# The end of an attention layer in a new order, and six of its sixteen output groups moved into the next layer's first steps

## The chip, the cores and the metric

The kernel runs on one core of a Trainium2 chip. The metric is device time in microseconds (us) of one launch. The engines are TensorE (PE for matmuls, PEld for weight loads), VectorE (DVE), ScalarE (ACT), GpSimd (POOL) and SyncE (SP, which issues the DMAs). All data is fp32.

## The reference

Four layers, each a gated cross-attention and a gated feed-forward network, are applied in turn to `x`, 128 batches of 64 tokens with 128 features (8192 tokens). The change lies between the two halves of layer 2 (the third layer):

```
x = x + tanh(g_xattn[2]) * L2_xattn(layernorm(x), ctx)     # 16 heads of 8, softmax over 64 keys
x = x + tanh(g_ffn[2])   * L2_ffn(layernorm(x))            # 32 experts

# L2_xattn:
q, k, v = x @ Wq + bq, ctx @ Wk + bk, ctx @ Wv + bv
attn = softmax(clip(q k^T / sqrt(8)))
attn = 1/64 everywhere if any attn is nan
out  = (attn v) @ Wo + bo

# L2_ffn: a sigmoid router picks 2 of 4 groups of experts, then the 8 best experts of these
final  = sum over chosen experts of w_e * down_e(silu(gate_e x) * up_e x)
shared = down_s(silu(gate_s x) * up_s x)
```

## The kernel before

`x` stays in SBUF for the whole kernel as 64 tiles of 128 tokens. A *pair* is two tiles (256 tokens, 32 pairs, numbers `u`), a *group* four tiles (512 tokens, 16 groups, numbers `g`). Group `g` holds pairs `2g` and `2g+1`.

The order of the instructions is written out by hand. Every engine is wrapped in `InOrder` (line 158), whose `issue` ties each instruction to the one issued before on that engine; so an engine runs its instructions in the order in which the Python code emits them, and all instructions carry line 166 in the profile. Work is told apart by the names of its tiles.

Layers are generators. While one layer ends, it calls `ahead().step()`, which runs the next layer's generator up to its next `yield`: this is how the first work of the next layer is put between the last work of this one. After a `yield False` a step does nothing more.

`l2_cross` (line 745) is the attention. Its `period(i)` (line 927) emits one step of a software pipeline over pairs by `PLAN` (line 920): scores, clamp, maximum, exponentials, `turn` (transposes of the attention, tile `aT`), `values` and `place` (the values into `vz`), `heads` (attention times values and the denominators, tile `pso_l2x`) and `divide` (a reciprocal and a product on DVE into `oT_all`). The tail begins when all 32 pairs have had their scores:

- `check` (line 949) counts NaNs in a sum of exponentials and leaves the flag `bad`. It needs all pairs' scores, so nothing may leave before it.
- `leave(g)` (line 958) is a `copy_predicated` on DVE, which puts the mean of the values into the group's part of `oT_all` where `bad` is set, and four 128x128 matmuls (two passes each) with `Wo` into a PSUM bank `psf`.
- `add(g)` (line 967) is one DVE instruction that adds the gated `psf` to `x`.
- `groups(lo, hi)` (line 971) emits `leave` for a run of groups, `add` two groups behind, and one `ahead().step()` after each add.

The three last `period` calls finish pairs 29, 30 and 31, with groups 0 to 4, 5 to 9 and 10 to 15 between and after them.

`l2_ffn` (line 990) is the expert layer. Its steps ahead are, for group 0: `statistics`, `norm`, `transposes`, `logits`, `sigmoid`, `groups`, `best_groups`, `best_experts`, `shares` and `spread` (the expert weights are transposed as `pswt`, copied as `wT` and written to DRAM by four DMAs, `wrow`), and then `statistics(1)` and `norm(1)`. The main part (line 1155) begins with `fetch(0)`: eight DMAs that spread the weights over all partitions as four 1 MB blocks `wb`, each for four steps. Then for every group there are 17 steps `j`, each with two experts (64 hidden features each), the last with the shared one:

- `hidden(g, j)`: the gate and up matmuls into a double bank `psgu` (two such buffers exist);
- `gated(g, j)`: `sl` on ACT (Silu), `uw` on DVE (up times weight `wb`), `h` on POOL (their product);
- `down(g, j-2)`: the down matmul into `psy`.

Between the steps stand the next group's router by the plan in line 1139 (`j` = 2 to 9) and the statistics of the group after it (`j` = 12 and 14). PSUM has four single banks (`psf`, `psy`, `psx`, `pswt`, ...) and two double ones. The buffers `sl`, `h`, `uw` take SBUF which `oT_all` had, so the first of them waits for its last use.

Of the kernel before, what the change touches and what calls it, by code (L numbers as in the profile page):

```python
# [9 lines left out]
F32 = mybir.dt.float32  # L10
U8 = mybir.dt.uint8
U32 = mybir.dt.uint32
AF = mybir.ActivationFunctionType
ALU = mybir.AluOpType
AX = mybir.AxisListType

P = 128
NB, SQ, DM = 128, 64, 128
DC = 96
NTOK = NB * SQ  # L20
NT = NTOK // P
NP = NT // 2
NG = NT // 4
# [31 lines left out]
def flamingo_kernel(ctx: ExitStack, tc: tile.TileContext, a: dict, out: bass.AP):  # L55
# [118 lines left out]
    def opened(name, bufs=1, side=None):  # L174
        pl = tc.tile_pool(name=name, bufs=bufs, side=side, reuse_waits="tile")
        return pl
# [17 lines left out]
    class Heads:  # L194
# [24 lines left out]
        def values(self):  # L219
            self.v = v = self.new("v", [P, 4, 256], bufs=3)  # L220
            for half in range(2):
                ps = bank(f"psv_{self.name}_{half}")
                for i in range(2):
                    b0 = self.p * 256 + (half * 2 + i) * SQ
                    for r in range(2):
                        self.pe.matmul(ps[r * 64:(r + 1) * 64, i * 256:(i + 1) * 256], lhsT=ctxT[0:self.vrows, b0:b0 + SQ],
                                       rhs=self.w["v"][0:self.vrows, self.off + r * 256:self.off + (r + 1) * 256],
                                       start=True, stop=True)
                self.act.copy(v[:, 2 * half:2 * half + 2, :].rearrange("p a b -> p (a b)"), ps)
# [39 lines left out]
        def power(self):  # L269
            s16 = self.s.rearrange("p a r k -> p (a r) k")  # L270
            self.act.activation(s16, s16, AF.Exp)

        def divide(self):
            s16 = self.s.rearrange("p a r k -> p (a r) k")
            den, rec = self.new("den", [P, 16]), self.new("rec", [P, 16])
            self.dve.tensor_reduce(den, s16, AX.X, ALU.add)
            self.dve.reciprocal(rec, den)
            self.at = self.s if self.null is None else self.new("at", [P, 8, 2, 64])
            self.pool.tensor_tensor(self.at.rearrange("p a r k -> p (a r) k"), s16[:, :, 0:64], bc(rec, 2, 64), ALU.mult)
# [462 lines left out]
                        W["l1x"] = weights("l1x", sp)  # L742


    def l2_cross(ahead):

        stack = ExitStack()
# [165 lines left out]
        def divide(u):  # L913
            rec = wk2.tile([P, 256], F32, tag="rec", name=f"rec_l2x_{u}", bufs=1)
            dve.reciprocal(rec, su[u]["o"][:, 256:512])
            dve.tensor_tensor(oT[:, u * 256:(u + 1) * 256], su[u]["o"][:, 0:256], rec, ALU.mult)
            su[u].clear()


# [7 lines left out]
        def period(i):  # L927
            for kind, lag, f, *more in PLAN:
                n = i + lag
                if 0 <= n < NP and (kind == "u" or n % 2 == 0):  # L930
                    f(n if kind == "u" else n // 2, *more)

        for i in range(-6, -1):
            period(i)
            yield i < -2

        one = stack.enter_context(opened("l2x_1"))
        W["l3x"] = weights("l3x")
        oT = one.tile([P, NTOK], F32, name="oT_all")
        cnt = one.tile([P, NT], F32, name="cnt")  # L940
        wk2 = late.enter_context(opened("l2x_2", 2))
        junk = wk2.tile([P, 1024], mybir.dt.bfloat16, name="junk", bufs=1)
# [1 line left out]
            period(i)  # L944
        early.close()

        bad, psf = one.tile([P, 1], U8, name="bad"), {}

        def check():

# [5 lines left out]
            dve.tensor_scalar(bad, ps[:, 0:1], float(P * NT), None, ALU.is_lt)  # L956

        def leave(g):
            og = oT[:, g * 512:(g + 1) * 512]
            dve.copy_predicated(og.rearrange("p (b q) -> p b q", q=SQ), bc(bad.to_broadcast([P, 8]), 2, SQ),  # L960
                                bc(vmT[:, 8 * g:8 * g + 8], 2, SQ))
            psf[g] = bank(f"psf_{g}")
            for t in range(4):
                cols = slice(t * P, (t + 1) * P)
                mat.matmul(psf[g][:, cols], lhsT=og[:, cols], rhs=w["o"], start=True, stop=True)

        def add(g):
            xs = x[:, 4 * g:4 * g + 4, :].rearrange("p t c -> p (t c)")
            dve.scalar_tensor_tensor(xs, psf.pop(g), tg[:, 2:3], xs, ALU.mult, ALU.add)

        def groups(lo, hi):
            for g in range(lo, hi + 2):
                if g < hi:
                    leave(g)
                if g >= lo + 2:
                    add(g - 2)
                    ahead().step()

        check()
        period(NP)  # L980
        groups(0, 5)
        period(NP + 1)
        groups(5, 10)
        period(NP + 2)
        groups(10, NG)
        late.close()
        stack.close()


    def l2_ffn(ahead):  # L990
# [3 lines left out]
        with opened("l2f_0", 2, RIGHT) as fr:  # L994
# [8 lines left out]
            def statistics(g):  # L1003
                sts, mv = new(g, "sts", [P, 4, 6]), new(g, "mv", [P, 4, 2])
                for t in range(4):
                    dve.bn_stats(sts[:, t, :], x[:, 4 * g + t, :])
                for t in range(4):
                    dve.bn_aggr(mv[:, t, :], sts[:, t, :])
                rs, rr = new(g, "rs", [P, 4]), new(g, "rr", [P, 4])
                gps.tensor_scalar(rs, mv[:, :, 1], EPS, None, ALU.add)  # L1010
                gps.tensor_tensor(rr, rs, nhalf, ALU.pow)

            def norm(g):
                xn = new(g, "xn", [P, 4, P], bufs=1)
                for t in range(4):
                    dve.tensor_scalar(xn[:, t, :], x[:, 4 * g + t, :], st[g]["mv"][:, t, 0:1], st[g]["rr"][:, t:t + 1],
                                      ALU.subtract, ALU.mult)
# [73 lines left out]
            def fetch(g):  # L1091
                wv = st[g]["wd"].rearrange("(j r) q -> r j q", r=2)
                for c in range(4):
                    wb = wbp.tile([P, 4, 512], F32, tag="wb", name=f"wb_l2f_{g}_{c}")
                    for r in range(2):
                        sp.dma_start(out=wb[r * 64:(r + 1) * 64], in_=wv[r, 4 * c:4 * c + 4].partition_broadcast(64))
                    st[g]["wb", c] = wb

            def hidden(g, j):

                xT = st[g]["xT"]
                wg, wu = (w[k][:, j * P:(j + 1) * P] for k in "gu") if j < 16 else (w["sg"], w["su"])
                gu = st[g]["gu", j] = banks(f"psgu_l2f_{g}_{j}")
                mat.matmul(gu[:, 0, :], lhsT=wg, rhs=xT, start=True, stop=True)
                mat.matmul(gu[:, 1, :], lhsT=wu, rhs=xT, start=True, stop=True)

            def gated(g, j):
                gu = st[g]["gu", j]
                sl = homes[False].tile([P, 512], F32, tag="sl", name=f"sl_l2f_{g}_{j}", bufs=3)
                actor.activation(sl, gu[:, 0, :], AF.Silu)  # L1110
                h = st[g]["h", j] = homes[False].tile([P, 512], F32, tag="h", name=f"h_l2f_{g}_{j}", bufs=3)
                if j < 16:
                    uw = homes[False].tile([P, 512], F32, tag="uw", name=f"uw_l2f_{g}_{j}", bufs=3)
                    dve.tensor_tensor(uw, gu[:, 1, :], st[g]["wb", j // 4][:, j % 4, :], ALU.mult)
                    gps.tensor_tensor(h, uw, sl, ALU.mult)
                else:
                    dve.tensor_tensor(h, gu[:, 1, :], sl, ALU.mult)
# [7 lines left out]
            def leave(g):  # L1125
                actor.copy(new(g, "ys", [P, 512]), st[g]["yo"])
# [6 lines left out]
            def add(g):  # L1133
                xs = x[:, 4 * g:4 * g + 4, :].rearrange("p t c -> p (t c)")
                dve.scalar_tensor_tensor(xs, st[g]["psback"], tg[:, 6:7], xs, ALU.mult, ALU.add)
                st[g].clear()
# [8 lines left out]
            for f in (statistics, norm, transposes, logits, sigmoid, groups, best_groups, best_experts, shares, spread):  # L1145
                f(0)
                yield True
            statistics(1)
            yield True
            norm(1)  # L1150
            yield False

            with opened("l2f_2", 2) as wk2, opened("l2f_wb", 4, RIGHT) as wbp:
                homes[False] = wk2
                fetch(0)
                for g in range(NG + 1):
                    for j in range(17):
                        if g >= NG - 1 and j % 3 == 1:
                            ahead().step()
                        if g < NG:  # L1160
                            hidden(g, j)
                            gated(g, j)

                        gd, jd = (g, j - 2) if j >= 2 else (g - 1, j + 15)
                        if 0 <= gd < NG:
                            down(gd, jd)
                        for lag, f in PLAN.get(j, ()):
                            if 0 <= g + lag < NG:
                                f(g + lag)
# [213 lines left out]
    def ahead(n):  # L1383
        return lambda: layers[n + 1]
# [113 lines left out]
```

## Time and profile before

| | |
|---|---|
| median of 3 runs | 3159.76 us (3157.87 to 3167.32) |
| the profiled execution | 3154.1 us, of which the profile's span is 3152.3 us |
| mean granted TensorE clock | 0.986 |
| attention of layer 2, first to last `oT_all` product | 1328.2 to 1619.4 us |
| flag `bad` known | 1577.3 us |
| last `psf` matmul starts | 1629.4 us |
| expert layer, first to last `psgu` matmul | 1629.5 to 2380.2 us |

All times on the trace are microseconds from the start of the span. A row of the timeline has a start, a length, the engine, the line, the operation with its output and inputs, and how often it is repeated in the row; in brackets stand the idle time of the engine before it, and what released it. Releasers are inferred from semaphores. The ends of matmuls are modelled. A window's row has the busy time of each engine in it with a count, then the granted clock of TensorE, the DMA engines' share and GB/s.

### The profile page before, as it was taken

What the parts mean: (1) busy time and instruction counts of PE and PEld (TensorE: products, weight loads), DVE (VectorE), ACT (ScalarE), POOL (GpSimd) and SP (SyncE); (2) the same over time, 40 slices, a digit from 0 to 9 for tenths busy, and PEclk for the clock granted to TensorE, in tenths of its full rate; (3) what the DMA queues carried; (4) which work ended last, traced back from release to release, by engine and by line L of the source; (5) the groups of instructions that cost most, each with busy time, mean ns of one, the idle gap of its engine ahead of it and who ended that gap; (6) DMA issues with size and microseconds to landing.
All of it is one profiled execution on the core that took longest, in us unless ns stands there. A gap on an engine that the chain in (4) does not pass through costs nothing. (4 is left out here: it accounts for less than half of the span.)

```text
span 3152.3 us, 80010 instructions
## 1 busy us (share of the span) xinstructions
PE 2984.2 (95%) x34018; PEld 1972.2 (63%) x34018; DVE 1935.9 (61%) x4558; ACT 1564.0 (50%) x2756; POOL 1261.6 (40%) x1439
## 2 busy tenths in 40 slices
PE   8999899999989999778879999999999999999998
PEld 7888544444448888555654444444446888888883
DVE  5666666666546667699964544544545666666664
ACT  5666432232236666688822332332325666666655
POOL 3434311111014444787714444444443333333343
PEclk9999999999999999899989999999999999999998
DMA  5000455655510000000025335435430000000001
GB/s 151 2 3 2 109 135 120 137 122 124 132 51 3 3 2 2 29 3 2 2 55 109 83 80 109 82 81 109 87 77 14 2 2 2 3 2 3 2 3 54
DMA packets 89512, 164.93 MB, mean 52 GB/s; under 512 B 8929, under 2 KB 20833, under 8 KB 88193
## 3 DMA queue, kind: packets, MB, share of 16 engines
q1 hardware_dynamic: 89154, 159.81, 22.6%
q8 instruction: 267, 4.37, 0.6%
q14 instruction: 91, 0.75, 0.1%
HBM read 154.00 MB, written 5.77 MB: 51 GB/s over the span
## 5 line engine op out<-in xcount | busy, mean ns | idle before, releaser
L166 PE MATMUL psgu_l2f<-xT_l2f,w_l2f 128*128 128x512 f32 x1088 | 512.7, 594 | 0.1
L166 POOL TENSOR_TENSOR h_l2f<-uw_l2f,sl_l2f 128x512 f32<-128x512 f32 x256 | 325.1, 1270 | 409.1 <-DVE uw_l2f L166 409.1
L166 DVE TENSOR_TENSOR uw_l2f<-psgu_l2f,wb_l2f 128x512 f32<-128x512 f32 x256 | 176.3, 689 | 361.6 <-ACT sl_l2f L166 361.6
L166 ACT ACTIVATE sl_l2f<-psgu_l2f 128x512 f32<-128x512 f32 x272 | 162.4, 597 | 465.9 <-PE psgu_l2f L166 465.8
L166 PE MATMUL psqkv_l0f<-xs_l0f,w_l0f 128*128 128x512 f32 (+1 forms) x1024 | 350.5, 599 | 3.5 <-DVE xs_l0f L166 3.5
L166 PEld LDWEIGHTS psgu_l2f<-xT_l2f,w_l2f 128*128 128x128 f32 x1088 | 202.1, 190 | 237.9 <-issue 222.6
L166 PE MATMUL psy_l2f<-h_l2f,w_l2f 128*128 128x512 f32 x544 | 277.6, 592 | 0.0
L166 PEld LDWEIGHTS psqkv_l0f<-xs_l0f,w_l0f 128*128 128x128 f32 (+1 forms) x1024 | 125.0, 164 | 188.9 <-issue 178.1
L166 POOL TENSOR_TENSOR at_l3x<-s_l3x,rec_l3x 128x1024 f32<-128x1024 f32 x64 | 121.8, 1904 | 164.3 <-DVE rec_l3x L166 153.6
L166 PEld LDWEIGHTS psy_l2f<-h_l2f,w_l2f 128*128 128x128 f32 x544 | 103.3, 190 | 129.6 <-issue 125.3
L166 POOL TENSOR_SCALAR rs_l0f<-mv_l0f 128x4 f32<-128x4 f32 x16 | 16.1, 1003 | 370.0 <-DVE mv_l0f L166 370.0
L166 DVE TENSOR_REDUCE den_l3x<-s_l3x 128x16 f32<-128x1040 f32 x64 | 79.1, 1235 | 130.1 <-ACT s_l3x L166 130.1
L166 POOL TENSOR_TENSOR x<-x,gbias_b 128x256 f32<-128x256 f32 (+1 forms) x80 | 68.0, 850 | 212.4 <-DVE ln_xn_l1x L166 109.1
L166 DVE TENSOR_TENSOR xs_l0f<-wb_l0f,xT_l0f 128x1024 f32<-128x1024 f32 x128 | 151.5, 1215 | 2.5 <-PE psqkv_l0f L166 1.1
L166 POOL TENSOR_TENSOR s_l2x<-s_l2x,m_l2x 128x1024 f32<-128x1024 f32 x64 | 120.4, 1903 | 53.4 <-DVE m_l2x L166 35.0
L166 PE MATMUL psq_l3x<-xT_l3x,w_l3x 128*128 128x256 f32 x512 | 135.3, 386 | 0.0
L166 PE MATMUL psk_l3x<-ctxT,w_l3x 96*128 96x256 f32 x512 | 132.4, 380 | 0.0
L166 PEld LDWEIGHTS pso_l3x<-w_l3x,oT_l3x 128*128 128x128 f32 x1024 | 125.9, 194 | 4.5 <-ACT oT_l3x L166 1.3
L166 DVE TENSOR_TENSOR s_l3x<-sc_l3x,maskf_m 128x512 f32<-128x512 f32 x128 | 82.4, 686 | 75.3 <-PE sc_l3x L166 75.3
L166 PE MATMUL pso_l3x<-w_l3x,oT_l3x 128*128 128x128 f32 x1024 | 126.4, 277 | 1.2 <-ACT oT_l3x L166 1.2
L166 PE MATMUL psv_l3x<-w_l3x,ctxT 97*64 97x256 f32 x1024 | 124.6, 385 | 0.0
L166 PE MATMUL psy_l0f<-mix_l0f,w_l0f 128*128 128x512 f32 x256 | 116.5, 609 | 2.0 <-DVE mix_l0f L166 2.0
(562 smaller groups left out, 6648.4 us busy)
## 6 DMA issues: line engine op xcount, KB each, us to landing
wb_l0f<-wrow_l0f SPq DMA_DIRECT2D x256, 256.0 KB, 5.7
wb_l2f<-wrow_l2f SPq DMA_DIRECT2D x128, 512.0 KB, 9.1
out_dram<-x SPq DMA_DIRECT2D x16, 256.0 KB, 2.6
w_l2f<-in_l2f_dram SPq DMA_DIRECT2D x1, 3280.0 KB, 10.3
w_l0f<-in_l0f_dram SPq DMA_DIRECT2D x1, 2088.0 KB, 27.5
w_l3x<-in_l3x_dram SPq DMA_DIRECT2D x1, 2049.0 KB, 8.3
x<-in_x_dram SPq DMA_DIRECT2D x1, 2048.0 KB, 18.9
ctxT<-in_ctxT_dram SPq DMA_DIRECT2D x1, 1536.0 KB, 23.7
```

The costliest lines, as they stand in the source:

```text
L166: got = getattr(self.eng, op)(*args, **kwargs)
```

## The change

The tail of `l2_cross` no longer calls `period` and `groups`. It is written out: the last three pairs (A = 29, B = 30, C = 31) are finished one after the other, with `leave` of groups 0, 1 and 2 between them; groups 3 to 9 leave after them, with the expert layer's twelve steps ahead between these. Groups 10 to 15 (`LATE = 6`) are put on a list. `l2_ffn` takes them from it in its group 0: at odd `j` (1, 3, ... 11) a `leave`, at the next even `j` its `add`. The tile `oT_all` is split in two, the second for the last six groups (`oT_rest`, in a pool that is kept to the end of the kernel). The hidden matmuls of the expert layer's first two steps are emitted ahead, with `statistics(1)` and `norm(1)`.

```
+    leaving, LATE = [], 6
...
-            dve.tensor_tensor(oT[:, u * 256:(u + 1) * 256], su[u]["o"][:, 0:256], rec, ALU.mult)
+            dve.tensor_tensor(heads_of(u // 2)[:, u % 2 * 256:(u % 2 + 1) * 256], su[u]["o"][:, 0:256], rec, ALU.mult)
...
+        rest = ctx.enter_context(opened("l2x_o"))
         one = stack.enter_context(opened("l2x_1"))
...
-        oT = one.tile([P, NTOK], F32, name="oT_all")
+        oTs = one.tile([P, (NG - LATE) * 512], F32, name="oT_all"), rest.tile([P, LATE * 512], F32, name="oT_rest")
+        bad = rest.tile([P, 1], U8, name="bad")
+
+        def heads_of(g):
+            late_, k = divmod(g, NG - LATE)
+            return oTs[late_][:, k * 512:(k + 1) * 512]
...
         def leave(g):
-            og = oT[:, g * 512:(g + 1) * 512]
+            og = heads_of(g)
...
+        A, B, C = NP - 3, NP - 2, NP - 1
         check()
-        period(NP)
-        groups(0, 5)
-        period(NP + 1)
-        groups(5, 10)
-        period(NP + 2)
-        groups(10, NG)
+        heads(A)
+        for t in range(2):
+            power(C, t)
+        leave(0)
+        values(B)
+        divide(A)
+        turn(B, 0)
+        add(0)
+        turn(B, 1)
+        ahead().step()
+        place(B)
+        heads(B)
+        leave(1)
+        values(C)
+        ahead().step()
+        divide(B)
+        turn(C, 0)
+        add(1)
+        turn(C, 1)
+        ahead().step()
+        place(C)
+        heads(C)
+        leave(2)
+        ahead().step()
+        add(2)
+        ahead().step()
+        divide(C)
+        leave(3)
+        for g in range(4, NG - LATE + 1):
+            ahead().step()
+            if g < 6:
+                ahead().step()
+            if g < NG - LATE:
+                leave(g)
+            add(g - 1)
+        while ahead().front:
+            ahead().step()
         late.close()
         stack.close()
+        for g in range(NG - LATE, NG):
+            leaving.append((g, leave, add))
...
             statistics(1)
+            hidden(0, 0)
             yield True
             norm(1)
+            hidden(0, 1)
             yield False
...
                 fetch(0)
+                last = []
                 for g in range(NG + 1):
                     for j in range(17):
...
                         if g < NG:
-                            hidden(g, j)
+                            if g or j > 1:
+                                hidden(g, j)
                             gated(g, j)
+                        if g == 0 and j % 2 == 1 and leaving:
+                            n, begin, end = leaving.pop(0)
+                            begin(n)
+                            last.append((n, end))
+                        if last and j % 2 == 0:
+                            n, end = last.pop()
+                            end(n)
 
                         gd, jd = (g, j - 2) if j >= 2 else (g - 1, j + 15)
                         if 0 <= gd < NG:
```

More of the change, by code (lines that the diff above doesn't have):

```diff
@@ L945, in l2_cross @@
         early.close()
-        bad, psf = one.tile([P, 1], U8, name="bad"), {}
+        psf = {}
         def check():
@@ L969, in add @@
             dve.scalar_tensor_tensor(xs, psf.pop(g), tg[:, 2:3], xs, ALU.mult, ALU.add)
[L971 to L977, printed above, removed]
-        check()
-        period(NP)
-        groups(0, 5)
-        period(NP + 1)
-        groups(5, 10)
-        period(NP + 2)
-        groups(10, NG)
+        A, B, C = NP - 3, NP - 2, NP - 1
+        check()
+        heads(A)
[35 more added lines that the diff above has]
+            ahead().step()
         late.close()
         stack.close()
+        for g in range(NG - LATE, NG):
+            leaving.append((g, leave, add))
     def l2_ffn(ahead):
```

## The prediction

> **What bounds the kernel now.** I read the page first (PE is busy 95% of the span), then the windows around the end of layer 2's attention, then the timeline there, because the change touches nothing else. The windows give start:end, length, busy time of each engine with its count, then the granted clock:
>
> ```profile
> PE 2984.2 (95%) x34018; PEld 1972.2 (63%) x34018; DVE 1935.9 (61%) x4558; ACT 1564.0 (50%) x2756; POOL 1261.6 (40%) x1439
> ...
> 1575.30:1629.50 54.20, 35.56 (x496) 31.23 (x497) 39.70 (x117) 9.13 (x16) 4.23 (x6) 0.82 0.20 43
> 1629.50:1674.00 44.50, 43.01 (x113) 18.92 (x112) 22.15 (x74) 13.90 (x24) 21.70 (x19) 1.00 0.53 108
> 1674.00:2330.00 656.00, 635.01 (x1673) 283.95 (x1672) 311.92 (x1023) 203.47 (x335) 299.99 (x263) 1.00 0.44 90
> ```
>
> The first window is the attention's tail, 54.2 us in which PE is busy 35.6 and DVE 39.7: neither is full. The second is the expert layer's group 0, where PE is full (43.0 of 44.5), as in the layer's other groups, the third window. So work taken out of the first window is cheap there, and work or a wait put into the second is paid whole. The timeline of the tail shows what ends its waits (bracket: idle before, releaser), then the start of the expert layer:
>
> ```profile
> 1581.42 1.00 DVE L166 COPY vz<-psv_l2x 64x128 f32<-64x128 f32 x4 [4.09 <-PE psv_l2x L166]
> 1598.21 1.00 DVE L166 COPY vz<-psv_l2x 64x128 f32<-64x128 f32 x4 [4.03 <-PE psv_l2x L166]
> 1617.61 1.76 DVE L166 RECIPROCAL rec_l2x<-pso_l2x 128x256 f32<-128x256 f32 x1 [3.57 <-PE pso_l2x L166]
> ...
> 1628.49 1.28 ACT L166 ACT_TABLE_LOAD   x1 [14.22 <-DVE oT_all L166]
> 1629.52 5.32 PE L166 MATMUL psgu_l2f<-xT_l2f,w_l2f 128*128 128x512 f32 x12
> 1632.07 0.69 DVE L166 TENSOR_TENSOR uw_l2f<-psgu_l2f,wb_l2f 128x512 f32<-128x512 f32 x1 [1.60 <-ACT sl_l2f L166]
> 1632.82 0.33 PEld L166 LDWEIGHTS psgu_l2f<-xT_l2f,w_l2f 128*128 128x128 f32 x2 [0.53 <-DVE uw_l2f L166]
> ```
>
> DVE waits three times, 11.7 us in all, for a pair's matmuls. The last line is the third expert step (j=2), at 1632.82: the mark I follow. The steady step further on:
>
> ```profile
> 1659.03 1.88 PE L166 MATMUL psgu_l2f<-xT_l2f,w_l2f 128*128 128x512 f32 x4
> 1660.74 1.02 PE L166 MATMUL psy_l2f<-h_l2f,w_l2f 128*128 128x512 f32 x2
> 1661.00 0.60 ACT L166 ACTIVATE sl_l2f<-psgu_l2f 128x512 f32<-128x512 f32 x1 [1.98 <-PE psgu_l2f L166]
> 1661.60 1.88 PE L166 MATMUL psgu_l2f<-xT_l2f,w_l2f 128*128 128x512 f32 x4
> 1661.63 0.69 DVE L166 TENSOR_TENSOR uw_l2f<-psgu_l2f,wb_l2f 128x512 f32<-128x512 f32 x1 [1.88 <-ACT sl_l2f L166]
> ```
>
> hidden takes 1.71 us, down 0.86, a step 2.57; and sl, uw come only after hidden has ended.
>
> **Part 1, the tail in a new order.** Removed from it: six groups' leave and add. On DVE a copy_predicated starts 0.62 after the one before it and an add 0.67, so 6 x 1.29 = 7.7 us. On PE 6 x 0.97 (24 psf matmuls of three groups last 2.92). Nothing is recomputed; the two oT tiles and heads_of issue nothing. I walk DVE and PE in the new order with these durations, from the flag at 1577.34. heads(29) ends at 1580.7 (half clock, as before), its reciprocal and product at 1583.0; turns, add(0), statistics(0), place(30) to 1586; heads(30), divide(30) to 1591; turn(31), heads(31), leave(2) on PE to 1596, where DVE waits about 4 us for psf(2), the longest wait of the new tail; divide(31) and leave(3) to 1600; the router's groups to shares (5.6 us) with leave(4) to 1608. pswt stands behind psf(5) on PE: about 1609.3, against 1613.53. ACT's wT (0.27) and SP's four wrow and eight wb DMAs move with it: wrow was issued 0.77 after pswt, wb 3.63 after that (1613.7), the quickest wb landed 5.0 after its issue, and a block's second half is issued 0.6 later, so that I take 6.3: 1620. SP holds nothing else here. POOL's rs, rr and mk move too; POOL stood idle 12 to 33 us there, so they cost nothing but the 0.6 us DVE waited for rr already. hidden(0,0) and hidden(0,1), 3.4 us of PE, now fit between leaves, where PE has gaps; without that cover they would cost 3.4. DVE is through with add(9) at about 1620, by this sum from 1577.3: 40.3 of old work (the old last add ended at 1630.5, 12.8 of it waits), less 7.7, plus some 10 of waits. The Silu table load (1.28) still follows the last use of oT_all, now cp(9) near 1616, and is hidden by the wb landing.
>
> So uw(0,0) starts at about 1620.3, uw(0,1) ends at 1621.7. Then cp(10): both its big operands are in SBUF, and POOL's h(0,0) is running by then. A row shows that price: eq beside h took 1.17 here against 0.23 in the tail:
>
> ```profile
> 1607.37 0.23 DVE L166 TENSOR_TENSOR eq_l2f<-eq_l2f,cst_t 128x64 f32<-128x64 f32 x1
> ...
> 1648.91 1.17 DVE L166 TENSOR_TENSOR eq_l2f<-eq_l2f,cst_t 128x64 f32<-128x64 f32 x1
> ```
>
> Between 0 and 1.2 us; I take 0.8, because h(0,0) runs for 1.26. cp(10) ends at 1623.2, psf(10) at 1624.3, and hidden(0,2), behind it on PE, starts at 1624.5. Gain 1632.8 - 1624.5 = 8.3 us, with about 2 us of doubt either way.
>
> **Part 2, leaves inside group 0.** At odd j the PE order becomes hidden(0,j), psf, down(0,j-2); the DVE order uw(0,j), copy_predicated. psf needs the copy, the copy stands behind uw, uw behind sl, sl behind this very hidden. Behind psf on PE stand down(0,j-2), whose h is long ready, and all later hidden. By the rows: hidden's end to sl 0.25, sl to uw 0.63, to the copy 0.62, the copy 0.72, to PE 0.1: PE stands 2.3 us, then works 0.97. For the five groups at j = 3 to 11: 5 x 3.27 = 16.4. At j=5 sl also waits for the two table loads around the sigmoid (sl came about 1.3 late before), which PE did not feel then: +0.7, the middle of 0 and 1.3. The adds at even j (0.67 of DVE) fit: DVE is busy half of this window. The bubble the router already makes in this group,
>
> ```profile
> 1656.31 0.30 PE L166 MATMUL pswt_l2f<-cst_t,wt_l2f 128*128 128x128 f32 x1 [1.49 <-DVE wt_l2f L166]
> ```
>
> stays, as uw(0,9) and cp(14) come on top of the same DVE queue. Sum +17.1. PE is full to the end of the layer and nothing behind it gives this back.
>
> **Part 3, the clock: the skill against the trace.** Row first, 3.4 us stretches in the old tail:
>
> ```profile
> 1601.30:1604.70 3.40, 2.46 (x22) 2.49 (x23) 3.27 (x11) 0.07 (x1) 0.00 (x0) 1.00 0.00 0
> 1604.70:1608.10 3.40, 1.62 (x13) 1.23 (x11) 3.26 (x21) 0.00 (x0) 0.00 (x0) 1.00 0.00 0
> 1608.10:1611.50 3.40, 2.05 (x8) 1.78 (x8) 3.33 (x18) 0.00 (x0) 0.00 (x0) 0.50 0.00 0
> ```
>
> The Trainium skill ("TensorE: Matmul & The Clock Gate", section "Why this matters for your kernels") says that the clock halves after a gap of more than some 3 us. By it, gaps of 2.3 us cost 0. The rows disagree: in the middle stretch no PE wait was over 1.6 us, PE was busy 1.62 of 3.40, and the next stretch ran at 0.50. A stretch that holds a whole 2.3 us gap is busy only 1.1. Each loss costs up to 1.7 us of PE, so five gaps lie between 0 (the rule) and 8.5 (the row, every time). Many gaps will straddle two stretches, and the 1.49 us gap above lost nothing; I take 2.
>
> **Part 4, memory.** The tile for the last six groups is kept to the end of the kernel (12 KB per partition), so later buffers move. It issues nothing; another old buffer may be waited for at the start of layer 3. The trace shows no such wait; bound -1 to +1, taken 0: PE's queue there is full anyway.
>
> **Sum.** -8.3 + 17.1 + 2 + 0 = +10.8 us. The profiled execution took 3154.1 (span 3152.3), which is 5.7 under the median of the runs; against its own time this gives 3164.9, against the median 3159.76 about 3170.5.
>
> **Rivals.**
> - **Leaves ride free.** If something keeps PE from standing at psf, only the work remains: -8.3 + 5 x 0.97 = -3.4, 3156.3; with no port wait and a tail 4 us shorter, -8 and below. The deciding point is a stall of (8.3 - 4.9) / 5 = 0.7 us per leave. For it: DVE has 50% free. Against: both queues run in written order, and the psf rows of the tail already show PE standing for oT_all. 0.2.
> - **Clock lost each time.** +8.8 + 8.5 = +17.3, 3177. For it the rows of part 3, against it the 656 us after at 1.00 with small gaps. 0.15.
> - **It does not do what it says:** the router chain or wb sets the start as before, so that the tail gains 3 us instead of 8.3: +16, 3176. Against: pswt is well ahead. 0.07.
> - The sum itself, 3165 to 3176: 0.58.
>
> **Numbers.** About 0.3% (9.5 us) is what a measurement of this kernel can tell from no change. The likeliest is 3170.5. The range, 3156 to 3182, reaches from the free ride to the clock rival plus some tail. Slower by over 0.3%: the rivals on the slow side, and a little over half of the main case: 0.54. Within: 0.37. Faster: the low end of the free ride, 0.09.
>
> **What would show it.** Right: five PE waits of 2 to 3 us before psf released by DVE oT_rest, group 0 near 60 us from its j=2 instead of 41, pswt near 1609, j=2 near 1624. Wrong: psf with waits under 0.7; or half clock in several stretches of group 0; or a first uw held by something other than wb or the adds.

## The result

The changed kernel takes 3180.28 us (median of 4 runs, 3176.79 to 3183.14), the kernel before 3158.82 us in the runs beside it (3156.72 to 3167.32). The ratio is 1.0058, with a 95% interval of 1.0043 to 1.0072: it is slower, by 18 us by the ratio (14 to 23 by its interval) and by 21 us by the medians. The forecast was 3170.5, in a range from 3156 to 3182; the result lies 1.7 us inside the upper end.

The profiled run took 3183.14 us, with a span of 3181.4. That is 29.1 us more than the profile of before, but 8.3 us of it lie ahead of anything that the change touches: `psnan`, the matmul of the flag, starts at 1584.9 here and at 1576.6 before. The start varies from run to run by that much: in the kernels below, which are the same up to there, `psnan` starts between 1579.3 and 1586.8. So stages are compared by two marks inside one profile: from the start of `psnan` to the first `uw_l2f` (the expert layer begins), and to the first `h_l2f` product on DVE, which is the shared expert at the end of group 0. The second is 1674.5 - 1576.6 = 97.9 us before, and 1701.3 - 1584.9 = 116.4 us now: +18.5. From there to the last `psgu` both kernels take the same 705.7 to 705.8 us. The rest of the expert layer gives nothing back.

The page of the changed kernel, first its engines, and then the window (start:end, length, busy time of each engine, granted clock) from its first `uw` to its shared expert:

```profile
PE 3001.4 (94%) x34018; PEld 1982.9 (62%) x34018; DVE 1938.2 (61%) x4558; ACT 1564.8 (49%) x2756; POOL 1263.4 (40%) x1439
...
1629.00:1701.30 72.30, 55.70 (x153) 27.84 (x154) 31.13 (x85) 12.92 (x21) 23.99 (x19) 0.86 0.42 85
```

The count of PE instructions is the same to the last one. In group 0 PE stands for 16.6 of 72.3 us, and the clock in it is 0.86 where it was 1.00. The windows further down show a clock of 1.00 or one half, so some 0.14 x 2 x 72.3 = 20 us of this one ran at half clock.

The timeline of the changed kernel from the end of the tail on shows where the expert layer begins:

```profile
1617.23 0.42 PE L166 MATMUL pswt_l2f<-cst_t,wt_l2f 128*128 128x128 f32 x1
1621.12 5.42 SPq L166 DMA_DIRECT2D wb_l2f<-wrow_l2f  x8
1624.20 1.28 ACT L166 ACT_TABLE_LOAD   x1 [6.24 <-DVE oT_all L166]
1628.97 1.29 DVE L166 TENSOR_TENSOR uw_l2f<-psgu_l2f,wb_l2f 128x512 f32<-128x512 f32 x2 [2.35 <-DMA wb_l2f<-wrow_l2f]
1630.18 1.41 DVE L166 COPY_PREDICATED oT_rest<-bad,vmT 128x512 f32<-128x512 uint8 x1
1631.74 2.05 PE L166 MATMUL psf<-w_l2x,oT_rest 128*128 128x128 f32 x8 [5.90 <-DVE oT_rest L166]
1633.58 3.60 PE L166 MATMUL psgu_l2f<-xT_l2f,w_l2f 128*128 128x512 f32 x4
```

The tail is indeed shorter. `uw(0,0)` starts 44.1 us after `psnan`, where it took 55.5 before, and what it waits for is the landing of `wb`. But PE has stood for 5.90 us when `psf(10)` starts, which then takes 2.05 (it takes 1.05 to 1.16 at full clock), and `hidden(0,2)` behind it takes 3.60 instead of 1.88. The other five late groups, in the same view:

```profile
1642.40 1.13 PE L166 MATMUL psf<-w_l2x,oT_rest 128*128 128x128 f32 x8 [2.20 <-DVE oT_rest L166]
1652.73 1.16 PE L166 MATMUL psf<-w_l2x,oT_rest 128*128 128x128 f32 x8 [3.39 <-DVE oT_rest L166]
1663.50 1.28 PE L166 MATMUL psf<-w_l2x,oT_rest 128*128 128x128 f32 x8 [2.76 <-DVE oT_rest L166]
1674.78 2.04 PE L166 MATMUL psf<-w_l2x,oT_rest 128*128 128x128 f32 x8 [3.30 <-DVE oT_rest L166]
1684.93 2.04 PE L166 MATMUL psf<-w_l2x,oT_rest 128*128 128x128 f32 x8 [2.20 <-DVE oT_rest L166]
```

Each one ends a wait for `oT_rest`, 13.85 us together. The windows of 3.4 us from the same stretch show what such waits do to the clock (the granted clock stands third from the end):

```profile
1657.70:1661.10 3.40, 3.04 (x8) 1.01 (x6) 2.21 (x4) 0.86 (x2) 1.26 (x1) 1.00 0.00 0
1661.10:1664.50 3.40, 1.00 (x8) 1.03 (x9) 3.26 (x8) 0.33 (x1) 1.65 (x1) 0.98 0.01 2
1664.50:1667.90 3.40, 3.40 (x7) 1.44 (x6) 1.21 (x13) 0.00 (x0) 0.00 (x0) 0.52 0.00 0
1667.90:1671.30 3.40, 3.40 (x9) 1.31 (x7) 1.68 (x3) 0.60 (x1) 0.91 (x1) 1.00 0.00 0
1671.30:1674.70 3.40, 0.17 (x1) 0.00 (x0) 3.12 (x9) 0.60 (x1) 0.99 (x2) 0.98 0.00 0
1674.70:1678.10 3.40, 3.32 (x10) 2.44 (x11) 0.00 (x0) 0.00 (x0) 1.02 (x1) 0.52 0.00 0
```

Every third stretch holds a wait (PE busy 1.00, then 0.17), and the stretch after it runs at half clock although PE is busy all through it.

### The profile page after: what moved, and what is told of

It reads as the page before. It is cut to its first block, busy times and chain, and to the rows that moved or that the text cites. A ratio compares the mean times of both kernels' runs of the same rounds, so it can differ in the third digit from the quotient of the medians.

```text
span 3181.4 us, 80012 instructions
## 1 busy us (share of the span) xinstructions
PE 3001.4 (94%) x34018; PEld 1982.9 (62%) x34018; DVE 1938.2 (61%) x4558; ACT 1564.8 (49%) x2756; POOL 1263.4 (40%) x1439
## 3 DMA queue, kind: packets, MB, share of 16 engines
q1 hardware_dynamic: 89154, 159.81, 22.4%
```

## The experiments

The theory after the result: PE stands at `psf` because its copy is queued behind `hidden`, `sl` and `uw` of the same step, and these waits also halve the clock in which the work behind them runs. The rivals: the work itself and DVE beside POOL cost the time; the tail's new order is at fault; moved buffers are; the clock is lost only while PE waits anyway. All marks, from single profiles, and the ratios to the kernel before with their 95% intervals:

| kernel | psnan to first uw | psnan to h_l2f | median us | ratio |
|---|---|---|---|---|
| before | 55.5 | 97.9 | 3158.82 | 1 |
| changed | 44.1 | 116.4 | 3180.28 | 1.0058 (1.0043 to 1.0072) |
| split | 43.9 | 99.7 | 3158.15 | 0.9994 (0.9985 to 1.0003) |
| early | 45.3 | 94.0 | 3154.49 | 0.9981 (0.9970 to 0.9992) |
| tail_only | 51.5 | 93.9 | 3158.04 | 0.9993 (0.9984 to 1.0003) |
| tiles_only | 55.4 | 97.9 | 3160.32 | 0.9998 (0.9988 to 1.0007) |
| filled | 43.9 | 106.7 | 3166.39 | 1.0023 (1.0010 to 1.0036) |
| three_late | 46.2 | 104.7 | 3164.20 | 1.0014 (1.0003 to 1.0024) |
| copies_ahead | 43.4 | 91.5 | 3153.90 | 0.9982 (0.9970 to 0.9994) |

The median of before in the runs beside the four kernels from split to tiles_only was 3159.52 us, beside the last three 3158.47 us.

### Tiles only: are moved buffers at fault?

The kernel before, with nothing but the change's two tiles:

```
+        LATE = 6
+        rest = ctx.enter_context(opened("l2x_o"))
         one = stack.enter_context(opened("l2x_1"))
...
-        oT = one.tile([P, NTOK], F32, name="oT_all")
+        oTs = one.tile([P, (NG - LATE) * 512], F32, name="oT_all"), rest.tile([P, LATE * 512], F32, name="oT_rest")
+        bad = rest.tile([P, 1], U8, name="bad")
...
```

> The kernel before with nothing but the attention output split in two tiles, the second kept to the end of the kernel, as in the change. Theory: no time up to layer 3 (97.9 us from psnan to h_l2f, within 0.5), and at most 2 us in layer 3, ratio 0.999 to 1.001. Rival (buffers that moved make layer 3 or the expert layer wait): ratio 1.002 or more.

Measured: 97.9 us between the marks, as before, and a ratio of 0.9998. The memory part of the change costs nothing that can be seen.

### Tail only: is the new order of the tail at fault?

The changed kernel, with all sixteen groups leaving in the tail:

```
-        for g in range(4, NG - LATE + 1):
+        for g in range(4, NG + 1):
...
-            if g < NG - LATE:
+            if g < NG:
                 leave(g)
...
-        for g in range(NG - LATE, NG):
-            leaving.append((g, leave, add))
```

> The changed kernel, but all sixteen groups leave in the tail; nothing is left for group 0. This is the new order of the tail and the early hidden alone. Theory: the tail's order is a gain of its own; 7.7 us of DVE come back, of which 2.35 fit in the wait for wb: 94 to 98 us from psnan to h_l2f (97.9 before), ratio 0.998 to 1.001. Rival (the tail's new order is what costs): over 102 us, ratio over 1.002.

Measured: 93.9 us, 4.0 less than before, just under the expected 94 to 98. Timeline of this kernel where the six groups leave:

```profile
1629.30 2.40 PE L166 MATMUL psf<-w_l2x,oT_rest 128*128 128x128 f32 x16 [0.68 <-DVE oT_rest L166]
1632.00 2.40 PE L166 MATMUL psf<-w_l2x,oT_rest 128*128 128x128 f32 x16 [0.30 <-DVE oT_rest L166]
1634.70 2.40 PE L166 MATMUL psf<-w_l2x,oT_rest 128*128 128x128 f32 x16 [0.30 <-DVE oT_rest L166]
1637.81 1.28 DVE L166 TENSOR_TENSOR uw_l2f<-psgu_l2f,wb_l2f 128x512 f32<-128x512 f32 x2
```

In the tail PE waits under 0.7 us for the same copies, because no `uw` stands ahead of them. The tail's order and the early `hidden` are a gain of 4 us; the moved leaves turn it into a loss of 18.5. So one late group costs (116.4 - 93.9) / 6 = 3.75 us more in group 0 than in the tail.

### Three late: is the price one for each group?

```
-    leaving, LATE = [], 6
+    leaving, LATE = [], 3
```

> The changed kernel with three late groups instead of six; three more leave in the tail. If each late group has the same price, (116.4 - 93.9) / 6 = 3.75 us over one that leaves in the tail, 105 us from psnan to h_l2f and a ratio near 1.003. Rival (the first is free under the wait for wb, and the price lies in the later ones): 101 to 103 us. Rival (one fixed price for entering the loop): over 110 us.

Measured: 104.7 us, (104.7 - 93.9) / 3 = 3.6 us for each late group. The price is one for each, and the wait for `wb` doesn't make the first one free. The ratio, 1.0014, came out lower than the 1.003 expected.

### Early copies: does psf stand only for its copy?

The changed kernel, with `leave` cut into `default` (the copy) and `project` (the matmuls); all six copies go to the tail and `project` stays where `leave` was:

```
+        for g in range(NG - LATE, NG):
+            default(g)
         late.close()
         stack.close()
         for g in range(NG - LATE, NG):
-            leaving.append((g, leave, add))
+            leaving.append((g, project, add))
```

> The changed kernel, but the six late groups' copies are all issued in the tail, before the expert layer's main part; psf stays at odd j directly behind hidden. Theory: psf has nothing to wait for, so PE pays only 0.97 us a group; the six copies (3.7 us of DVE) partly fill the 2.35 us in which DVE waits for wb: 96 to 100 us from psnan to h_l2f, ratio 0.998 to 1.002. Rival (the place of psf between hidden and down, or the work, costs): 108 us or more.

Measured: 94.0 us, less than the 96 to 100 expected, and a ratio of 0.9981, whose interval lies below 1. Its timeline:

```profile
1640.18 1.05 PE L166 MATMUL psf<-w_l2x,oT_rest 128*128 128x128 f32 x8
1646.22 1.05 PE L166 MATMUL psf<-w_l2x,oT_rest 128*128 128x128 f32 x8
1652.27 1.05 PE L166 MATMUL psf<-w_l2x,oT_rest 128*128 128x128 f32 x8
1654.50 0.30 PE L166 MATMUL pswt_l2f<-cst_t,wt_l2f 128*128 128x128 f32 x1 [0.32 <-DVE wt_l2f L166]
```

No bracket: `psf` at the same place between `hidden` and `down` waits for nothing, and takes 1.05. (Only the first of the six, which PE reaches in the tail, still waits 1.57 us, and the first `hidden` of the loop runs at half clock, 3.78.) The same PE work, the same adds in group 0; 22.4 us less between the marks. Only the place of the six copies differs, and so it is the cause of the loss. The last line shows a gift: the wait for the router's `wt`, 1.49 us before, is down to 0.32, since the leaves ahead of it fill that time.

### Split: one step later

The copy at odd `j`, its matmuls at the next step behind that step's `hidden`, the add one step after:

```
-                        if g == 0 and j % 2 == 1 and leaving:
-                            n, begin, end = leaving.pop(0)
-                            begin(n)
-                            last.append((n, end))
-                        if last and j % 2 == 0:
-                            n, end = last.pop()
-                            end(n)
+                        if g == 0 and j % 2 == 1:
+                            if last:
+                                n, project, end = last.pop()
+                                end(n)
+                            if leaving:
+                                n, begin, project, end = leaving.pop(0)
+                                begin(n)
+                                last.append((n, project, end))
+                        if g == 0 and j % 2 == 0 and last:
+                            n, project, end = last[0]
+                            project(n)
```

> The changed kernel, but each late group's copy_predicated is issued at odd j, its psf matmuls one step later behind the next hidden, its add one step after that. Same work, same engines. Theory (PE stands at psf behind hidden, sl, uw and the copy, and these gaps halve the clock): the psf waits fall from 2.2 to 3.4 us to under 0.3, group 0 shows no half clock after its start, and from the flag's matmul psnan to the first shared-expert product h_l2f on DVE it takes 96 to 99 us (97.9 before, 116.4 in the changed kernel); the ratio to before is 0.998 to 1.001. Rival (the added work itself, on PE and on DVE beside POOL, is what costs): at least 108 us and a ratio of 1.004 or more.

Measured: 99.7 us, 0.7 over the expected. The waits were not all gone, and behind the longest of them `hidden` ran at half clock, which the expectation had excluded:

```profile
1645.83 1.16 PE L166 MATMUL psf<-w_l2x,oT_rest 128*128 128x128 f32 x8 [2.10 <-DVE oT_rest L166]
1648.07 3.20 PE L166 MATMUL psgu_l2f<-xT_l2f,w_l2f 128*128 128x512 f32 x4
1654.76 1.13 PE L166 MATMUL psf<-w_l2x,oT_rest 128*128 128x128 f32 x8 [0.92 <-DVE oT_rest L166]
1662.03 1.13 PE L166 MATMUL psf<-w_l2x,oT_rest 128*128 128x128 f32 x8 [0.51 <-DVE oT_rest L166]
1669.14 1.16 PE L166 MATMUL psf<-w_l2x,oT_rest 128*128 128x128 f32 x8 [0.83 <-DVE oT_rest L166]
```

One step of 2.57 us is hardly more than the 2.3 us from the end of `hidden` to the end of the copy, so that anything more on DVE or ACT shows. Here DVE has more: in this version the add of the group before stands ahead of the copy, and the copy, which then starts while POOL's `h` runs, takes 1.35 us where it took 0.72 in the changed kernel:

```profile
1643.77 0.74 DVE L166 SCALAR_TENSOR_TENSOR x<-psf,tg,x 128x512 f32<-128x512 f32 x1
1643.93 1.26 POOL L166 TENSOR_TENSOR h_l2f<-uw_l2f,sl_l2f 128x512 f32<-128x512 f32 x1 [4.06 <-DVE uw_l2f L166]
1644.42 1.35 DVE L166 COPY_PREDICATED oT_rest<-bad,vmT 128x512 f32<-128x512 uint8 x1
```

The expectation missed both.

### Filled: is the lost clock a cost of its own?

The changed kernel, with matmuls that nobody needs in front of each late `psf`, into the bank which `psf` then overwrites:

```
+        def busy(g):
+            default(g)
+            psf[g] = bank(f"psf_{g}")
+            for _ in range(6 if g == NG - LATE else 2):
+                mat.matmul(psf[g], lhsT=ident, rhs=W["l2f"]["g"][:, 0:512], start=True, stop=True)
+            project(g, psf[g])
...
-            leaving.append((g, leave, add))
+            leaving.append((g, busy, add))
```

> The changed kernel, with idle matmuls added: right before each late group's psf PE runs two more 128x512 matmuls (six before the first) into the psf bank, which psf then overwrites. They need nothing, and at full clock take 1.7 us of the 2.2 to 3.4 us that PE stands there. The chain to psf and its place are the same. Theory with the clock as a large part (in the changed kernel group 0 had 20 us at half clock from its start on): half clock disappears from group 0 except at most one stretch, and from psnan to h_l2f it takes 107 to 111 us instead of 116.4. Rival (the clock loss is harmless because PE waits anyway): 115 us or more, though 13 matmuls of work were only added.

Measured (these are 6 + 5 x 2 = 16 matmuls, not 13): 106.7 us, 9.7 less than the changed kernel and just under the expected 107 to 111. The window from the first `uw` to the shared expert, and of the timeline the first late `psf` with `hidden(0,2)` behind it, and two later groups, each with its idle matmuls first:

```profile
1629.30:1692.20 62.90, 57.45 (x179) 27.23 (x178) 31.16 (x85) 12.93 (x21) 23.99 (x19) 1.00 0.48 99
...
1632.01 1.16 PE L166 MATMUL psf<-w_l2x,oT_rest 128*128 128x128 f32 x8 [0.55 <-DVE oT_rest L166]
1633.00 1.88 PE L166 MATMUL psgu_l2f<-xT_l2f,w_l2f 128*128 128x512 f32 x4
...
1656.52 1.88 PE L166 MATMUL psf<-w_l2f,cst_t 128*128 128x512 f32 x4
1659.35 1.16 PE L166 MATMUL psf<-w_l2x,oT_rest 128*128 128x128 f32 x8 [0.95 <-DVE oT_rest L166]
1665.49 1.88 PE L166 MATMUL psf<-w_l2f,cst_t 128*128 128x512 f32 x4
1668.87 1.16 PE L166 MATMUL psf<-w_l2x,oT_rest 128*128 128x128 f32 x8 [1.49 <-DVE oT_rest L166]
```

The chain to `psf` is as long as it was: behind the first late group, filling (1.71 us each) and the wait left over take 2.1 to 3.4 us, 13.4 in all where the waits took 13.85. But the clock is 1.00 all through, and the kernel with more work is faster by 9.7 us. That is the price of the clock, apart from the wait.

### Copies ahead: a version that beats both

Three copies in the tail, where DVE waits 2.35 us for `wb`, and the others at `j` = 1, 3, 5, six steps before their matmuls:

```
+        for g in range(NG - LATE, NG - 3):
+            default(g)
...
-            leaving.append((g, leave, add))
+            leaving.append((g, default, project, add))
...
-                            n, begin, end = leaving.pop(0)
-                            begin(n)
+                            if len(leaving) > 3:
+                                leaving[3][1](leaving[3][0])
+                            n, begin, project, end = leaving.pop(0)
+                            project(n)
```

> The changed kernel, but the copies run three late groups ahead of their psf: those of groups 10 to 12 in the tail, as in the run with early copies, those of 13 to 15 at j = 1, 3, 5, six steps before their psf. DVE's three tail copies (1.9 us) fit in its 2.35 us wait for wb, where six (3.7 us) did not. Theory: the first uw comes 1 us sooner than with six early copies (44.1 instead of 45.3 after psnan) and PE still never stands at psf: 92.5 to 94 us from psnan to h_l2f (94.0 with six), ratio 0.997 to 0.9985, the best of all. Rival (copies beside POOL in the loop delay uw): 95 us or more.

Measured: 91.5 us, 6.4 less than before, 25 less than the changed kernel, and less than the 92.5 to 94 expected. Its timeline at the start:

```profile
1627.61 1.95 DVE L166 COPY_PREDICATED oT_rest<-bad,vmT 128x512 f32<-128x512 uint8 x3
1630.19 1.29 DVE L166 TENSOR_TENSOR uw_l2f<-psgu_l2f,wb_l2f 128x512 f32<-128x512 f32 x2 [0.63 <-DMA wb_l2f<-wrow_l2f]
1630.94 3.62 PE L166 MATMUL psgu_l2f<-xT_l2f,w_l2f 128*128 128x512 f32 x4 [1.34 <-DVE uw_l2f L166]
1637.40 1.05 PE L166 MATMUL psf<-w_l2x,oT_rest 128*128 128x128 f32 x8
```

The three copies lie in the wait, of which 0.63 us are left. The ratio, 0.9982, is not told apart from that of the early copies by its interval; only the marks inside the profiles put it 2.5 us ahead. Both are faster than the kernel before, by about 0.2%. The first late `psf` still waits 1.57 us for its copy in the tail, and the first `hidden` of the loop runs at half clock (3.62): there is a little left to gain.

## Why the prediction was right, and where its sum was not

The direction, the mechanism and most of its places were right; one term, the clock, was too small by a factor of nearly five. The range held the result because it was drawn out to the clock rival: 3180.28 lies above the main case (3165 to 3176) and above that rival's 3177. Of the signs named for right, the five waits, `pswt` and the start of `j` = 2 came as forecast (1608.9 and 1625.3, when the later start of this profile, 8.3 us, is taken off). But group 0 took 67.7 us from its `j` = 2, not 60, and one of the signs named for wrong came too: half clock in several stretches of group 0.

- **The start.** Forecast: `pswt` 32.8 us after `psnan` (1609.3 - 1576.5), `uw(0,0)` at 43.8, `hidden(0,2)` 8.3 us earlier. Measured: 32.4, 44.1, and (1633.58 - 1584.9) against (1632.82 - 1576.6), 7.5 earlier. With the waits filled it is 8.7 earlier (1633.00 - 1585.45): most of what is missing is `psf(10)` at half clock. Named rightly: the landing of `wb` ends the wait, with the table load under it. The copy beside POOL took 1.41 instead of 0.72, 0.7 more where 0.8 was taken.
- **The waits at psf.** Forecast: 5 x 2.3 and 0.7 for the table loads, 12.2 us. Measured: 13.85. The quickest two are 2.20, as the rows gave; the one behind the table loads is 3.39. In those of 2.76 and 3.30 the next group's router, which the forecast left out here, stood ahead of `uw` on DVE: `uw` started 0.6 and 1.1 us after its `sl` had ended. With 5 x 0.97 of work this term is 18.7 instead of 17.1.
- **The router's bubble.** Forecast: it stays. Measured: the leaves swallow it, a gain of some 1.5 us that the sum missed. In the changed kernel `pswt` waits for nothing.
- **The clock.** Forecast: 2 us, between 0 by the rule and 8.5 by the row. Measured by filling the waits: 9.7. This is the term that failed, in two places: of the five gaps counted, four lost the stretch behind them, where 2 us is little more than one loss; and the wait at `psf(10)` was not counted at all, though in the forecast's own walk PE has nothing between `psf(9)`, which must end before the add at about 1620, and `psf(10)` at about 1623.3. Windows of the changed kernel, laid on the steps at which its clock changes:

```profile
1630.21:1633.62 3.41, 1.88 (x9) 1.91 (x10) 1.38 (x2) 0.00 (x0) 2.48 (x2) 0.50 1.05 211
1633.62:1637.04 3.42, 3.42 (x6) 1.35 (x6) 0.00 (x0) 0.00 (x0) 0.00 (x0) 0.50 1.06 207
...
1640.45:1643.86 3.41, 1.46 (x10) 1.19 (x10) 1.33 (x2) 0.44 (x1) 1.65 (x1) 1.00 0.64 127
1643.86:1647.28 3.42, 3.42 (x16) 1.35 (x15) 0.00 (x0) 0.79 (x2) 0.00 (x0) 1.00 0.02 5
...
1654.10:1657.52 3.42, 3.42 (x5) 1.35 (x4) 1.23 (x17) 0.00 (x0) 0.00 (x0) 0.50 0.00 0
...
1681.41:1684.82 3.41, 1.32 (x4) 0.25 (x2) 2.15 (x4) 0.60 (x1) 1.86 (x2) 1.00 0.51 110
1684.82:1688.24 3.42, 3.31 (x10) 2.54 (x11) 0.00 (x0) 0.00 (x0) 1.05 (x1) 0.50 1.04 213
```

  The first two are the loss behind the wait of 5.90 us. With these, 1654.10, 1684.82 and the two in the windows of the result, six stretches ran at half clock. PE was busy 18.7 us in them, so that the loss is some 9.3 us by estimate, 2.7 of it in the first two. The row of before (a stretch busy 1.62 of 3.40 lost the next one) had the right answer, and the choice near the rule had not: by the rule of the Trainium skill ("TensorE: Matmul & The Clock Gate", "Why this matters for your kernels") only the waits of 5.90, 3.30 and 3.39 us could have lost the clock, but those of 2.76 and, at 1684.93, of 2.20 lost it too. What was taken for a saving, that many gaps would straddle two stretches, saved one loss at most (behind the wait that ends at 1642.40): a round of two steps with a late group lasts 10.2 to 11.3 us, about three stretches, so that the later waits keep falling into the same place of the pattern.
- **Memory.** Forecast: 0. The tiles alone show 0.2 parts in a thousand, within the interval.

In sum: with the clock at 1.00, the run with filled waits is 106.7 - 97.9 = 8.8 us over before, against 8.8 in the forecast without its clock term. That the two agree so closely is partly luck: the longer waits and the router's bubble, 1.6 more and 1.5 less, cancel. With the clock it is 18.5. The rival that has the clock lost each time (+17.3) was the better description. Of the 21.5 us between the medians, 18.5 lie before the end of group 0. From the first `psn_l3x` to the last `psh_l3f` the changed kernel's profile has 2.3 us more (758.2 against 755.9), but kernels with the same buffers had 750.3 to 758.0, one profile each: whether this is the change or the run stays open.

The rival of leaves that ride free was not far off as a design: with their copies ahead, the gain is 6.4 us, more than the 3.4 that it forecast.

## What to carry to other kernels

Work moved beside a full engine is free only if what it waits for is ready when its turn comes: in a queue that runs in order, put the producer well ahead of the consumer, not into the same step. Here one step ahead left waits of 0.4 to 2.1 us and six steps ahead left none; what lies between was not measured. Before moving work into a full loop, write down for every engine what stands ahead of the moved instruction, and count the way through the other engines as a wait of the full one. And a wait of the tensor engine is to be priced twice: by its length, and by the clock of the stretch that follows.

## What the hardware showed

- In this part of the kernel the clock went by how long PE was busy in fixed stretches of 3.41 us, and not by the length of a gap. From 1555 to 1710 us, in the nine traces, all 27 stretches at full clock with PE busy up to 1.43 us were followed by half clock, and none of the 296 with 1.75 us or more; of the 13 between, ten were. So of two waits of 2.20 us one lost the clock (1.32 us busy in its stretch) and one did not (1.46). These figures don't hold for the whole kernel: near its end, where matmuls of other shapes run, a stretch with 2.57 us busy (from 3116.78 in the kernel before) was followed by half clock too.
- A loss behind a wait of 2.2 to 3.4 us lasted one stretch, since PE was busy nearly all through it; behind the wait of 5.90 it lasted two. Together the losses cost 9.7 us in 72.
- DVE's copy of two SBUF operands took 1.35 to 1.42 us when it started while POOL's `h` ran, and 0.72 when it started first or alone. In the changed kernel five copies started 0.16 to 0.17 us before `h`; then the copy took 0.72, and `h` 1.65 instead of 1.27.
- Sixteen matmuls with no use, some 13.8 us of PE work at 0.86 each, made the kernel faster by 9.7 us between the marks; the medians are 3166.39 and 3180.28.
